# Recurrent layer of a four-layer graph network: two multiplies behind a bank's read, and the output's side steps at other places of length 4

## The chip, the cores and the metric

The kernel runs on one core of a Trainium2 chip. The core has five engines with a queue of instructions each: TensorE (PE, matrix products), VectorE (DVE), ScalarE (ACT), GpSimd (POOL) and SyncE (SP, which here issues nearly all DMA transfers). The metric is the device time of one execution in microseconds, from three runs of each kernel.

## What is computed

The input x has 128 batch rows of 64 nodes with 256 features, in fp32. Four layers follow each other, each as x = layernorm(x + layer(x)): a graph attention layer, an attention layer over an edge list, a layer with two batch norms, and the recurrent layer, which the change concerns:

```
h = relu(adj @ (x @ Wg0 + bg0)); h = relu(adj @ (h @ Wg1 + bg1))
for p in 1..4:
    wins = h in windows of p nodes            # nw = 64 // p windows per batch row
    LSTM p (zero initial state) over the p nodes of each window
    h[last node of each window] = the LSTM's last hidden state
x = layernorm(x + h)
```

An LSTM step is i, f, g, o = x_t @ Wih.T + h @ Whh.T + bias; c = sigmoid(f)*c + sigmoid(i)*tanh(g); h = sigmoid(o)*tanh(c). In length p there are p steps, and the first has no f and no h. "Length 4" is p = 4: four steps of 16 windows. It writes only the last node of each window of four, so nodes 0, 1 and 2 of each window are final before length 4 begins.

## The kernel before

**Groups and pairs.** The recurrent layer handles the batch in 8 groups of 16 rows, two groups (n = 0, 1) at a time: four pairs, k = 0 to 3, one after the other. Within a pair, `lstm(k)` runs lengths 1 to 4. The state is transposed (features on partitions), H is the pair's array of hidden values.

**Seven products.** A gate needs a 2 by 2 block product: feature halves by groups. It is done with seven products in place of eight (Strassen's scheme), with sums of weights (in `wx`, `wh`), of inputs (`xs`) and of hidden values (`hs`), the last two made by DVE and POOL. In lengths 2 to 4 each product j of a gate has an input half (`H` or `xs` by `wx`) and a hidden half (`hid` or `hs` by `wh`), which accumulate in one PSUM bank (L1700). "f.6" below is product 6 of gate f. The banks are a ring of six tiles named `l`, reused in the order of their allocation. Each product's result is read out of its bank by `use`: products 1 and 5 by a copy on ACT (L1715, into `kept`), 2 (L1717), 6 (L1719), 7 (L1721), 4 (L1726) and 3 (L1728) by an addition on DVE. Product 7 has two more additions without PSUM (L1723, L1724), on POOL for f, g and i, on DVE for o. A gate takes its products in the order 1, 5, 2, 6, 7, 4, 3; gate f takes 1, 5, 6, 7, 3, 2, 4; gate o takes 1, 5, 2, 6, 7, 3, 4. Then ACT applies sigmoid or tanh (L1733), and `finish` updates the cell (L1610 on POOL for f, L1613 and L1614 on DVE for i).

**A step's end.** Behind gate o come the input halves of the next gate f (products 1, 5, 6, 7, 3, 2, which fill the six banks), the hidden values (L1600) and their sums: L1564 and L1565 on DVE, L1568 and L1569 on POOL. Then gate f's hidden halves.

**Units.** `lstm` is a generator that stops at numbered places ("at" u, and some "gap" and "wait" places beside them). In length 4: 33 and 34 lie behind gates g and i of step 0, 35 at the end of step 0; 36, 37, 38 behind gates f, g, i of step 1, 39 at its end; 40 to 43 the same for step 2; 44 to 46 behind f, g, i of step 3, and 47 at the end. Two kinds of side work are put at units by `put`:

- `final(g, s)` puts out the nodes s = 0, 1, 2 of group g's windows; it has two halves. The first: x3r is loaded, POOL copies from H to `hd` (L1835), DVE transposes in blocks (L1236), SP sends the result to DRAM (`way<-st`, L1239) and back in four transfers (`st<-way`, L1241). The second: DVE adds x3r (L1850) and takes the norm's sums (L95, L96, L85, L98), POOL the power (L86) and the scaling (L100), SP the output (L1860).
- `gcn` makes the next pair's H, in blocks of 11 or so parts: a fetch of z from DRAM with the same kind of transposition, norms, two matrix layers (L1324 with L1326 on DVE and L1328 on ACT, L1336 with L1339 on DVE) and a last part that writes H (neighbour products L1254, L1347 on DVE, L1348 on ACT). Pair 3 has no next pair, and so none of this.

**Order.** All this is traced through `given`, which keeps the instructions of PE, DVE, ACT and POOL in the order written, but for a few neighbours within one part; each engine's queue is that order. SP's order is a scheduler's.

**Length 1.** Each gate is a `Wide` object, for group n; its products share three banks, so product 4 can only accumulate when the read of 7 (`add(room, b, self.first)`) is done. What a gate leaves over is its `tail`, run between the products of the next gate (`seven`): the first part behind product 1, and so on, in the order 1, 6, 5, 2, 3, 7 (o of group 1: 1, 6, 5, 2, 7, 3). `after(m, v)` multiplies: i by g, or o by tanh of the cell into H. Most DVE work of length 1 is shown under one line, L116, that of the helper which calls it.

Of the kernel before, what the change touches and what calls it, by code (L numbers as in the profile page):

```python
# [41 lines left out]
def kernel(ctx: ExitStack, tc: tile.TileContext, i, out):  # L42
# [67 lines left out]
    def given(do, *args, **more):  # L110
        traced = nc.cur_bb.bb.instructions
        first = len(traced)
        with ExitStack() as order:
            for e in latest.values():
                order.enter_context(tc.issue_after(e))
            r = do(*args, **more)  # L116
        for t in traced[first:]:
            if t.engine in (mybir.EngineType.PE, mybir.EngineType.DVE, mybir.EngineType.Activation,
                            mybir.EngineType.Pool):
                latest[t.engine] = t  # L120
        return r
# [8 lines left out]
    with ExitStack() as two:  # L130
# [605 lines left out]
        def hidden(q, m):  # L736
            return Z[q][:, m, :] if m < 2 else Aq(q)[:, (m - 2) * QT:(m - 1) * QT]
# [15 lines left out]
        def put(q, m, p_):  # L753
            nc.scalar.activation(hidden(q, m), p_, AF.Identity, bias=b1[:, m:m + 1])
            nc.vector.bn_stats(st1[:, m, q, :], hidden(q, m))
# [40 lines left out]
        class Seven:  # L796
# [57 lines left out]
            def tail(self):  # L854
                self.product(4)
                yield self.counted(1, 1)
                yield self.counted(1, 0)
                if self.done:
                    self.order(self.done)
# [114 lines left out]
        def load_x2(q):  # L974
            tiles = []
            for a in range(2):
                tiles.append(wx.tile([P, 2, D], F32, name="x2r"))
                nc.sync.dma_start(tiles[a].rearrange("p c d -> p (c d)"), x2_dram[q][:, a * 2 * D:(a + 1) * 2 * D])
            return tiles

        early = {n: load_x2(n) for n in range(2)}
# [110 lines left out]
        rest = late.pop(0).tail()  # L1092
# [37 lines left out]
        rest = late.pop(0).tail()  # L1130
# [101 lines left out]
    def turned(src):  # L1232


        t = work.tile([P, 4, 4, 32], F32, name="st", bufs=ST)
        nc.vector.transpose(t, src.rearrange("p n (j t) -> p j n t", t=32))  # L1236
        o = work.tile([P, 4, 4, 32], F32, name="st", bufs=ST)
        way = dram.tile([P, 4, P], F32, name="way", bufs=4)
        nc.sync.dma_start(way, t.rearrange("p j n f -> p j (n f)"))  # L1239
        for j in range(4):  # L1240
            nc.sync.dma_start(o[j * 32:(j + 1) * 32].rearrange("t i n f -> t i (n f)"),  # L1241
                              way[:, j, :].rearrange("(i t) x -> t i x", t=32))
        return o.rearrange("p i (c m) f -> p c m i f", m=KD)
# [132 lines left out]
    def lstm(pair):  # L1376
# [19 lines left out]
        class Wide:  # L1396
# [71 lines left out]
                if self.name == "i":  # L1468
                    given(nc.scalar.activation, self.t[m][v], self.t[m][v], AF.Tanh)

            def tail(self):
                self.act(0, 1)
                yield
                self.after(0, 0)
                self.after(0, 1)
                yield
                self.product(4)
                self.act(1, 1)
                yield
                self.act(1, 0)  # L1480
                self.tanh(0, 0)
                yield
                self.after(1, 0)
                self.after(1, 1)
                self.tanh(0, 1)
                yield
                self.tanh(1, 1)
                self.tanh(1, 0)

# [10 lines left out]
        def eight(G, rest):  # L1500

            def two(m, v):
                b = lbank([QT])
                for k in range(KD):
                    nc.tensor.matmul(b, G.weight(m, k), half(G.n, k, v), start=k == 0, stop=k == KD - 1)
                return b

            for m in range(2):
                for v in range(2):
                    G.act(m, v, given(two, m, v))  # L1510
                    next(rest, None)
            for _ in rest:
                pass

        def seven(G, rest, order):
            for j in order:
                G.product(j)
                next(rest, None)
            for _ in rest:
                pass  # L1520

        rest = iter(())
        for n in range(2):
            if n == 0:
                given(column_sums, 0)
                yield "begin", 0
            gates = {}
            for name in "gio":
                if (n, name) == (0, "o"):
                    given(column_sums, 1)  # L1530
                G = Wide(name, n, gates)
                if name == "g" and n == 0:
                    eight(G, rest)
                    rest = iter(())
                else:
                    seven(G, rest, (1, 6, 5, 2, 7, 3) if (n, name) == (1, "o") else (1, 6, 5, 2, 3, 7))
                    rest = G.tail()
                if (n, name) == (1, "o"):
                    G.last()
                yield "at", unit  # L1540
                unit += 1
            yield "at", unit
            unit += 1

        for p in range(2, SKIP + 1):
# [197 lines left out]
            for r in range(len(runs)):  # L1743
                if p > 2:
                    yield "gap", unit
                for s in range(p):
                    last = s == p - 1
                    if s == 0:
                        tiles = {}
                        free, rest = late_columns(r)  # L1750
# [12 lines left out]
                    else:  # L1763
                        names = "fgio"
                        for at, n in enumerate(names):
                            G = nxt or Gate(n, r, s, tiles)
# [61 lines left out]
    def final(g, s, pieces=1):  # L1828

        if s == SKIP - 1:  # L1830
            h = lasts.pop(g)
        else:
            h = late.tile([P, 2, KD, P], F32, name="hd", bufs=3)
            for c in range(2):
                nc.gpsimd.tensor_copy(h[:, c].rearrange("p k (w b) -> p k w b", b=GB),  # L1835
                                      Hs[g // 2][:, g % 2].rearrange("p k (c w s) b -> p c k w s b",
                                                                     c=2, s=SKIP)[:, c, :, :, s, :])

        rows = [v[g * GB:(g + 1) * GB].rearrange("b (c w s) d -> s c w b d", c=2, s=SKIP)[s]
                for v in (x3_dram, out_view)]  # L1840
        xr = work.tile([P, 2, D], F32, name="x3r")
        for c in range(2):
            nc.sync.dma_start(xr[:, c, :], rows[0][c])
        for cs in ([(0, 1)] if pieces == 1 else [(0,), (1,)]):
            r = slice(cs[0], cs[-1] + 1)
            if pieces == 1:
                ht = turned(h.rearrange("p c m t -> p (c m) t"))
                yield
                xv = xr.rearrange("p c (m i f) -> p c m i f", m=KD, f=32)
                nc.vector.tensor_add(xv, ht, xv)  # L1850
            else:
                ht = gbank([2, D])
                for c in cs:
                    for k in range(KD):
                        nc.tensor.transpose(ht[:, c, k * P:(k + 1) * P], h[:, c, k], ident)
                nc.vector.tensor_add(xr[:, r], ht[:, r], xr[:, r])
            o = work.tile([P, 2, D], F32, name="st", bufs=ST)
            layernorm(o[:, r], xr[:, r], len(cs), nc.gpsimd)
            for c in cs:
                nc.sync.dma_start(rows[1][c], o[:, c, :])  # L1860
        yield
# [32 lines left out]
    def gap(u):  # L1894
        return "gap", u

    def wait(u):
        return "wait", u

    for k in range(NP):  # L1900
        if k:
            put(k, prepare(weights_of[k, 3]), 8)
            put(k, prepare(weights_of[k, 4]), 23)
        else:
            put(k, prepare(weights_of[k, 4]), 23, 26, 30)
        for n in range(2):
            g = k * 2 + n
            for s in range(SKIP - 1):
                u = 34 + 4 * s + 2 * n
                put(k, final(g, s), u, u + 2)  # L1910
            if k < NP - 1:
                put(k + 1, final(g, SKIP - 1), 9 + n, 12 + n)
        if k < NP - 1:
            put(k, prepare(weights_of[k + 1, 2]), 34)
            for n, keys in enumerate([
                    [9, gap(11), 12, wait(15), 16, gap(18)],
                    [5, 9, 11, 13, 15, 19, wait(22), gap(22), gap(25), 26, gap(29)],
                    [13, 17, 19, 21, 23, 27, wait(33), gap(33), gap(36), 37, 38],
                    [21, 24, 26, 28, 30, 34, gap(40), 41, gap(44), 45, 46]]):
                block = gcn((k + 1) * 2 + n // 2, n % 2, gbank, "hT")  # L1920
                if n == 0 and k:
                    put(k - 1, block, 40, 42, 43)
                    put(k, block, 0, 0)
                elif n == 0:
                    put(k, block, 0, 1, 3, 5, 7)
                put(k, block, *keys)
# [48 lines left out]
```

## Time and profile before

| what | us |
|---|---|
| median of 3 runs | 2053.97 (2053.06 to 2055.26) |
| profiled execution | 2051.53 |
| its span, first to last instruction | 2049.7 |
| TensorE busy | 1943.6 (95%) |
| DVE, ACT, POOL busy | 1256.3, 987.6, 883.8 |
| mean granted TensorE clock | 0.986 of full speed |

The recurrent layer takes from about 797 us to the end, some 312 us for each pair but the first and last (pair 1 from 1133 to 1445 us). A timeline line reads: start, duration, engine, source line, operation, written tile <- read tiles, shapes, count; in brackets the idle time of that engine just before it and who ended it. Lines of a table of waits read: who waited, for whom: us in total, how often, the longest. The name of a line in the profile (L1700) is a line of the kernel; behind the edited places lines of the changed kernel stand four further on, or three.

### The profile page before, as it was taken

What the parts mean: (1) busy time and instruction counts of PE and PEld (TensorE: products, weight loads), DVE (VectorE), ACT (ScalarE), POOL (GpSimd) and SP (SyncE); (2) the same over time, 40 slices, a digit from 0 to 9 for tenths busy, and PEclk for the clock granted to TensorE, in tenths of its full rate; (3) what the DMA queues carried; (4) which work ended last, traced back from release to release, by engine and by line L of the source; (5) the groups of instructions that cost most, each with busy time, mean ns of one, the idle gap of its engine ahead of it and who ended that gap; (6) DMA issues with size and microseconds to landing.
All of it is one profiled execution on the core that took longest, in us unless ns stands there. A gap on an engine that the chain in (4) does not pass through costs nothing.

```text
span 2049.7 us, 31505 instructions
## 1 busy us (share of the span) xinstructions
PE 1943.6 (95%) x11447; PEld 1332.9 (65%) x11447; DVE 1256.3 (61%) x2763; ACT 987.6 (48%) x1892; POOL 883.8 (43%) x1017
## 2 busy tenths in 40 slices
PE   5999999999899989899999999999999999999997
PEld 4666667766454435477677477677577667578685
DVE  7456665564457454765566865556775557764566
ACT  2766667666335633634343644343544333544333
POOL 1123334343345543564545543435443445444264
PEclk8999999999999999999999999999999999999998
DMA  5344443332112125432242243132143032131022
GB/s 134 79 65 68 79 69 54 66 50 39 37 29 60 41 103 171 158 136 98 112 143 85 77 140 139 42 126 91 52 153 120 21 113 65 44 119 78 0 65 70
DMA packets 236539, 173.84 MB, mean 85 GB/s; under 512 B 150624, under 2 KB 213600, under 8 KB 233056
## 3 DMA queue, kind: packets, MB, share of 16 engines
q1 hardware_dynamic: 234528, 169.86, 29.1%
q8 instruction: 90, 1.47, 0.3%
q0 software_dynamic: 1024, 1.05, 0.2%
q10 hardware_dynamic: 832, 0.92, 0.1%
q14 instruction: 65, 0.53, 0.1%
HBM read 110.18 MB, written 61.60 MB: 84 GB/s over the span
## 4 chain that ended last, share of the span: by engine, by line
PE 68%; DVE 17%; ACT 5%; POOL 4%; issue 4%; DMA 1%; SPq 0%; DVEq 0%; POOLq 0%; ACTq 0%
PE l L1700 25%; PE l L1656 7%; PE l L1437 4%; PE pz L820 4%; PE e L346 3%; PE m L318 2%; PE pz L749 2%; PE g L1336 2%; PE m L253 2%; PE m L321 2%; PE z L355 2%; PE pz L1017 2%; PE g L1324 2%; DVE ln_st L95 1%; DVE cell L1614 1%
## 5 line engine op out<-in xcount | busy, mean ns | idle before, releaser
L1700 PE MATMUL l<-xs,wx 128*128 128x256 f32 (+1 forms) x896 | 277.0, 400 | 5.7 <-DVE gate L1719 4.2
L1700 PE MATMUL l<-hs,wh 128*128 128x256 f32 (+1 forms) x896 | 276.5, 399 | 2.9 <-DVE hs L1564 2.1
L1715 ACT ACTIVATE kept<-l 128x256 f32<-128x256 f32 (+1 forms) x224 | 88.6, 402 | 332.2 <-PE l L1700 330.7
L86 POOL TENSOR_TENSOR ln_rs<-ln_rs,mhalf 128x2 f32<-128x2 f32 (+2 forms) x98 | 86.4, 882 | 338.1 <-DVE ln_rs L98 334.9
L1700 PE MATMUL l<-H,wx 128*128 128x256 f32 (+1 forms) x672 | 210.5, 402 | 4.3 <-DVE gate L1728 3.4
L1700 PE MATMUL l<-hid,wh 128*128 128x256 f32 (+1 forms) x672 | 208.8, 399 | 0.0
L1700 PEld LDWEIGHTS l<-xs,wx 128*128 128x128 f32 x896 | 168.6, 190 | 50.7 <-issue 5.8
L1700 PEld LDWEIGHTS l<-hs,wh 128*128 128x128 f32 x896 | 169.2, 190 | 46.8 <-DVE hs L1564 4.7
L1733 ACT ACTIVATE gate<-gate,bias 128x512 f32<-128x512 f32 (+1 forms) x280 | 170.6, 657 | 42.0 <-DVE gate L1724 34.8
L1656 PE MATMUL l<-H,wx 128*128 128x256 f32 (+5 forms) x672 | 185.2, 431 | 4.9 <-DVE H L116 2.7
L1656 PEld LDWEIGHTS l<-H,wx 128*128 128x128 f32 x672 | 118.8, 190 | 65.5 <-issue 34.2
L357 ACT ACTIVATE u<-z 128x1024 f32<-128x1024 f32 x128 | 130.3, 1025 | 63.4 <-PE z L355 62.6
L1700 PEld LDWEIGHTS l<-H,wx 128*128 128x128 f32 x672 | 125.7, 190 | 42.6 <-DVE gate L1728 7.4
L1700 PEld LDWEIGHTS l<-hid,wh 128*128 128x128 f32 x672 | 127.2, 190 | 32.0 <-issue 2.6
L1723 POOL TENSOR_TENSOR gate<-gate,kept 128x256 f32<-128x256 f32 (+1 forms) x84 | 64.9, 773 | 154.2 <-DVE kept L1721 153.9
L329 DVE TENSOR_TENSOR qs<-m,qs 64x256 fp32r<-64x256 f32 x128 | 54.1, 422 | 109.1 <-ACT qs L328 107.0
L355 PE MATMUL z<-gath_r,qs 128*128 128x512 f32 x256 | 99.9, 478 | 0.6 <-ACT u L357 0.4
L1622 ACT ACTIVATE gate<-cell 128x512 f32<-128x512 f32 (+1 forms) x88 | 58.6, 666 | 86.5 <-DVE cell L1614 64.5
L1568 POOL TENSOR_TENSOR hs<-hid 128x256 f32<-128x256 f32 (+1 forms) x28 | 27.4, 977 | 168.3 <-DVE hid L1600 85.2
L1728 DVE TENSOR_TENSOR gate<-l,gate 128x256 f32<-128x256 f32 (+1 forms) x112 | 50.0, 446 | 61.4 <-POOL gate L1723 36.4
L1610 POOL TENSOR_TENSOR cell<-gate,cell 128x512 f32<-128x512 f32 (+1 forms) x56 | 75.4, 1367 | 28.4 <-ACT gate L1733 28.4
L1717 DVE TENSOR_TENSOR gate<-l,kept 128x256 f32<-128x256 f32 (+1 forms) x112 | 49.2, 439 | 57.1 <-ACT gate L1733 32.9
(375 smaller groups left out, 4095.3 us busy)
## 6 DMA issues: line engine op xcount, KB each, us to landing
wx<-sums SPq DMA_DIRECT2D x9, 2048.0 KB
wh<-sums SPq DMA_DIRECT2D x9, 1792.0 KB
way<-st SPq DMA_DIRECT2D x54, 256.0 KB
st<-way SPq DMA_DIRECT2D x216, 64.0 KB
xin<-in_x SPq DMA_DIRECT2D x16, 512.0 KB
ld<-table SPq DMA_DIRECT2D x16, 512.0 KB
x_dram<-y SPq DMA_DIRECT2D x16, 512.0 KB
x2r<-x_dram SPq DMA_DIRECT2D x32, 256.0 KB
```

Source lines behind the costliest of these rows:

```text
L86: nc.gpsimd.tensor_tensor(dst, dst, mhalf[:, :n], OP.pow)
L346: nc.tensor.matmul(pes[S][n * CG:(n + 1) * CG, :], apad[:, k, CG - HEADS - r0:2 * CG - HEADS - r0], u[:, k, :], start=r0 == 0 and k == 0, ...
L355: nc.tensor.matmul(z[:, k, :], L1[q]["qs"][c][:, s, k * P:(k + 1) * P], gath_r, start=True, stop=True)
L357: nc.scalar.activation(u, z, AF.Relu)
L820: nc.tensor.matmul(self.bank[at], lhs, rhs, start=first and n == 0, stop=n == len(self.terms) - 1, skip_group_check=True)
L1437: nc.tensor.matmul(self.bank[at], lhs, rhs, start=new, stop=True, skip_group_check=True)
L1610: nc.gpsimd.tensor_tensor(c, t, c, OP.mult)
L1656: nc.tensor.matmul(b, w.raw[0][:, k, at, m, :], x, start=k == 0, stop=k == KD - 1)
L1700: nc.tensor.matmul(self.banks[j], lhs, rhs, start=src == 0, stop=src == 1)
L1715: nc.scalar.activation(self.keep(j), b, AF.Copy)
L1723: e.tensor_tensor(t[0][:, 1], t[0][:, 1], k[5], OP.add)
L1733: given(lambda: nc.scalar.activation(dst, dst, f, bias=b))
```

## The change

In length 1, `tail` gets an argument. For every gate but i of group 1, the two multiplies `after(1, 0)` and `after(1, 1)` move from the fifth part (behind product 3 of the next gate) to the sixth (behind product 7, so behind the read of it). For gate g they do nothing; for i of group 0 they are the products i*g, for o of group 0 the writes of H.

In length 4, the places of the side steps change. The halves of `final`, by group n and node s:

| block | first, second half before | after |
|---|---|---|
| n = 0, s = 0 | 34, 36 | 33, 35 |
| n = 1, s = 0 | 36, 38 | 35, 37 |
| n = 0, s = 1 | 38, 40 | 36, 39 |
| n = 1, s = 1 | 40, 42 | 39, 41 |
| n = 0, s = 2 | 42, 44 | 40, 43 |
| n = 1, s = 2 | 44, 46 | 43, 44 |

The last part of the third `gcn` block of the next pair moves from 38 to 39, and the two fetches of the first block of the pair after that from 42 and 43 to 43 and 45. No instruction is added or removed.

```diff
-            def tail(self):
+            def tail(self, early):
                 self.act(0, 1)
                 yield
                 self.after(0, 0)
@@
                 self.act(1, 0)
                 self.tanh(0, 0)
                 yield
-                self.after(1, 0)
-                self.after(1, 1)
+                if early:
+                    self.after(1, 0)
+                    self.after(1, 1)
                 self.tanh(0, 1)
                 yield
+                if not early:
+                    self.after(1, 0)
+                    self.after(1, 1)
                 self.tanh(1, 1)
                 self.tanh(1, 0)
@@
-                    rest = G.tail()
+                    rest = G.tail((n, name) == (1, "i"))
@@
             for s in range(SKIP - 1):
-                u = 34 + 4 * s + 2 * n
-                put(k, final(g, s), u, u + 2)
+                put(k, final(g, s), *((33, 35), (35, 37), (36, 39), (39, 41), (40, 43), (43, 44))[2 * s + n])
@@
-                    [13, 17, 19, 21, 23, 27, wait(33), gap(33), gap(36), 37, 38],
+                    [13, 17, 19, 21, 23, 27, wait(33), gap(33), gap(36), 37, 39],
@@
                 if n == 0 and k:
-                    put(k - 1, block, 40, 42, 43)
+                    put(k - 1, block, 40, 43, 45)
                     put(k, block, 0, 0)
```

## The prediction

> **What bounds the kernel now.** I read the page first: busy time and the slices.
>
> ```profile
> span 2049.7 us, 31505 instructions
> PE 1943.6 (95%) x11447; PEld 1332.9 (65%) x11447; DVE 1256.3 (61%) x2763; ACT 987.6 (48%) x1892; POOL 883.8 (43%) x1017
> PE   5999999999899989899999999999999999999997
> ```
>
> TensorE sets the time; in the recurrent layer (from 797 us on) nearly every slice is full. So an edit elsewhere counts only where it makes PE wait or ends a wait. Next the table of waits:
>
> ```profile
> DVE st L1236 <- POOL hd L1835: 41.8, 20, 3.3
> PE l L1700 <- DVE gate L1719: 4.2, 6, 1.0
> PE l L1700 <- DVE gate L1728: 3.4, 8, 0.4
> ```
>
> PE's waits in lengths 2 to 4 are a few us in all: little is to be won there. DVE waits 41.8 us for the copies of the output's side steps, at no cost to PE. Why not? The timeline after gate f of step 1, second pair of groups (unit 36):
>
> ```profile
> 1364.97 0.88 DVE L1850 TENSOR_TENSOR x3r<-st,x3r 128x512 f32<-128x512 f32 x1
> 1367.05 0.15 DVE L98 TENSOR_SCALAR ln_rs<-ln_mv 128x2 f32<-128x2 f32 x1
> 1367.87 0.70 POOL L86 TENSOR_TENSOR ln_rs<-ln_rs,mhalf 128x2 f32<-128x2 f32 x1
> 1368.67 1.09 POOL L100 TENSOR_SCALAR st<-x3r,ln_rs 128x256 f32<-128x256 f32 x2
> 1369.70 0.74 POOL L1835 COPY hd<-H 128x256 f32<-128x256 f32 x2
> 1370.47 0.71 DVE L1236 STREAM_TRANSPOSE st<-hd 128x512 f32<-128x512 f32 x1 [3.27 <-POOL hd L1835]
> ```
>
> Here one output block's second half (add, norm) is followed by the next block's first half (copies, transpose). DVE sends its sums to POOL, POOL does power, scaling, copies, and DVE stands until the copies end. From L86 to the transpose is 2.6 us. PE goes on because all six `l` banks are filled in turn and gate g's products are ahead of DVE; DVE's next read (g.2, product 2 of g) ends about 1371.5, and PE wants that bank for i.5 at 1372.63. The margin is about 1 us. In the last pair the same place already costs PE 0.49 us.
>
> The step end of step 1 (unit 39):
>
> ```profile
> 1389.60 0.42 DVE L1564 TENSOR_TENSOR hs<-hid 128x256 f32<-128x256 f32 x1
> 1390.06 0.83 DVE L1565 TENSOR_TENSOR hs<-hid,hs 128x256 f32<-128x256 f32 x1
> 1390.96 0.69 DVE L1326 TENSOR_TENSOR hT<-g,rb 128x512 f32<-128x512 f32 x1
> 1391.68 0.63 ACT L1328 ACTIVATE hT<-hT 128x512 f32<-128x512 f32 x1 [2.66 <-DVE hT L1326]
> 1392.22 0.64 ACT L1715 ACTIVATE kept<-l 128x256 f32<-128x256 f32 x2
> 1392.61 0.42 DVE L1719 TENSOR_TENSOR gate<-l,kept 128x256 f32<-128x256 f32 x1 [0.97 <-ACT kept L1715]
> 1393.34 0.59 PE L1700 MATMUL l<-xs,wx 128*128 128x256 f32 x2
> 1395.07 0.60 PE L1700 MATMUL l<-xs,wx 128*128 128x256 f32 x2
> ```
>
> At a step end all six banks hold gate f's input halves, so PE has little to do without readers: f.4 (1393.34) takes f.1's bank, which ACT empties (L1715); g.1 takes f.5's; g.5 (1395.07) takes f.6's, which DVE empties (L1719, done 1393.03). Margin: 2.0 us for DVE, 0.5 us for ACT.
>
> **What the Trainium skill says.** "TensorE: Matmul & The Clock Gate", architectural detail: ACT, DVE and GpSimd queues are strict first in, first out, so an instruction that waits holds all behind it; the 3.27 us above agree. "SBUF — State Buffer", who interferes with whom: DVE and GpSimd share a port pair as a lock; the trace agrees (L1565 takes 0.83 us beside a POOL operation, 0.38 in another place). "DMA: Bandwidth & Descriptors", anatomy of one DMA: about 2 us fixed per transfer; a block's two transfers in a row would be at least 4 us. The trace's number is used: from the transpose's end to landing 7.3 to 8.7 us where x3r loads go between (1371.2 to 1379.9; 2022.2 to 2029.7).
>
> **The change, part by part.**
>
> *Length 1.* Before, DVE does two products i*g (1.3 to 2.2 us) ahead of the read of o.7, and PE waits for that read: 1.12 us in pairs 1 to 3, 0.53 in pair 0. Moved behind it, this wait goes. But ACT's tanh needs the products, and ACT's copy of the next group's g.1 is queued behind tanh; PE needs that copy 1 us later (matmul at 1156.59, copy done 1156.54). The products start 0.35 us later (o.7's 0.68 less the present wait for ACT); bounds 0, where POOL's lock sets their end anyway, and +0.4. I take +0.2 in three pairs and +0.4 in pair 0. The same move for o's products saves in pair 0 alone: PE waits 1.77 us for the add of g.7, which can run 1.5 us earlier. Sum about -0.5 us.
>
> *Length 4, what leaves.* Units 38, 42, 46 (behind gate i) lose their side work, so DVE reaches the cell products sooner. That can end PE's gaps ahead of the step ends: 0.34+0.43 and 0.24+1.02+0.43 us in pair 1, a little less in pairs 0 and 2, 0.46+0.43 and 0.45+0.43 in pair 3. The neighbour products (64 records, 1.16 us) moved from unit 38 to 39 cost PE the same there; their two writes of H go along, L1347 on DVE and L1348 (1.06 us) on ACT, whose only reader is the next pair. The first block for the pair after next moves its two fetches from 42 and 43 to 43 and 45: at 43 the same L1268, L1236 and transfers as now, at 45 another, read two gates and seven us of length 1 later: nothing. In the tail DVE waits 1.14 us for a landing and does 1.9 us of norm ahead of L1613; L1613 can then start when ACT's gate is ready, 2030.9 instead of 2031.74: -0.8.
>
> *Length 4, what arrives.* In the changed program's order, units 35, 39 and 43 have on DVE: L1564, the add L1850 (ahead of L1565 at 39 and 43), statistics, the transpose L1236, and only then gate f's reads; on POOL: power, scaling, copies, and only then L1723 of f.7. The double block that waited behind f now stands ahead of f.
>
> Unit 39, pair 1. DVE's chain comes up to 2.4 us earlier (neighbours gone from 38, no side work): L1564 at 1387.2. Then L1850 to 1388.3, L1565 to 1389.1, statistics 1.55 us to 1390.65, POOL to transpose 2.6 us, transpose to 1394.0, L1347 (the block's write of H, moved here) to 1394.9, L1326 to 1395.6. ACT's L1328 needs L1326 and stands ahead of the copies of f.1 and f.5: 0.63+0.38, 1396.6. PE wants f.1's bank at 1393.34-0.8 = 1392.5: it stands 4.1 us, and after the 0.8 gained the net is +3.3.
>
> Unit 35, pair 1: L1565 done 1359.16; add and statistics to 1361.4; transpose 1364.1 to 1364.8; L1339 to 1365.4; f.6 read at 1365.85. PE wants it at 1364.86: +1.0, and 0.1 where POOL is late for f.3: +1.1. Nothing on ACT waits here.
>
> Unit 43, pair 1: chain 1.6 us earlier, L1564 at 1418.1; L1850, L1565 to 1419.7; statistics 1421.2; transpose 1423.9 to 1424.6; L1236 of that block's fetch and L1339 to 1426.0; f.6 read 1426.4. PE wants it at 1425.16-1.7 = 1423.5: 2.9, net +1.2. Then unit 44: the second half of the block whose first half was at 43. Only the five reads of f lie between, done at 1429; the landing is due 7.3 to 8.7 us after 1424.6, 1431.9 to 1433.3. DVE stands there, then add, statistics and g.2: 2.65 us, 1434.5 to 1435.9. PE wants g.2's bank for i.5 at 1434.15: 0.4 to 1.8, taken as 1.1. Net +2.3.
>
> Sum 6.7 us a pair, pairs 0 to 2 alike: 20.1.
>
> Pair 3 has no next layers to fill PE. Unit 33: the transpose comes ahead of L1616, and the copies end at 1952.05 where L1616 now starts 1950.67: hid and hs come 2.1 us later, PE's margin is 1: +1.1, +0.5 for L1565; then f.6 read at 1965.9 for g.5 wanted 1963.4: +2.5; unit 36's own wait +0.6. Together +4.7. Unit 39: g.5 at 1990.9 instead of 1989.30, +1.6, and i.5 at unit 40 +0.5: +2.1. Units 43, 44: +1.6, then landing 2025.2 to 2026.6, g.2 read 2027.9 to 2029.2, i.5 wanted at 2024.45: 3.4 to 4.8, taken as 4.1: +5.7. Tail -0.8. Sum +11.7.
>
> All: -0.5+20.1+11.7 = +31 us on the profiled execution's own 2051.5 us (span 2049.7), 1.5%. The median of runs is 2.5 us above that execution; the same addition gives 2085. DMA issues are the same in number; SP's order moves with them, and its issue times (0.3 to 0.65 us) lie inside the landings used.
>
> **The rivals.**
> A, faster: the bank ring covers the step ends as it covers unit 36 now, and the gaps ahead of them vanish: about -2 us in each of four pairs, -0.8 in the tail, -0.5 in length 1: -9, 2045. It decides at f.6 read less than 2.0 us later and ACT's copies less than 0.5 us later. For it: 41.8 us of DVE waits cost PE almost nothing today. Against: I count 3.3 to 5.9 us.
> B, small loss: statistics and POOL overlap more than in my chain, and unit 44's landing comes in time. Only the ACT wait at 39 (3.3 x 3) and half of pair 3 (6) remain: +16, 2070.
> C, large loss: transfers land late behind each other and L1339's buffer waits for an output's DMA at 43; 1.5 us more at each of 12 step ends: +49, 2103.
> D, no change: gains and stalls cancel, 2054.
>
> **How the numbers follow.** Forecast 0.56, B 0.22, C 0.10, A 0.08, D 0.04. A measurement tells a change from none at about 0.2%, 4 us. Faster 0.08, same 0.04, slower 0.88. The range leaves out A and D and the far half of C: 2058 to 2102. The likeliest case alone: 2074 to 2096.
>
> **What would show it.** Right: PE gaps behind every step end of length 4, at f.4 (released by ACT L1715) in unit 39 of the first three pairs, at g.5 (by DVE L1719) elsewhere; DVE waiting for L1835 ahead of gate f; DVE waiting for st<-way in unit 44, 1 to 5 us; 1.12 us before o.4 gone, with a wait for ACT at g.2 in its place. Wrong: PE without gaps over 1 us behind the step ends, or the new losses sitting in another length.

## The result, and the profile after

The changed kernel takes 2090.99 us (median of 4 runs, 2088.02 to 2095.23) against 2054.48 us of the kernel before beside it, 36.5 us more. Their ratio was measured as 1.0183, with a 95% interval of 1.017 to 1.0196. On 2051 us that ratio is 37.5 us, and the table of the experiments below reckons every ratio so. The prediction said 2085 (2058 to 2102). The profiled execution has a span of 2086.2 us, 36.5 more than before.

The page of the kernel after, its first lines:

```profile
span 2086.2 us, 31516 instructions
PE 1953.2 (94%) x11447; PEld 1338.5 (64%) x11447; DVE 1256.5 (60%) x2763; ACT 988.7 (47%) x1892; POOL 876.3 (42%) x1017
PE   5999999998999989899999999999999999999986
```

The slices look as before: a loss of 1.8% doesn't show in tenths. One number does: DVE, ACT and POOL are as busy as before within 8 us, yet TensorE's busy time grew by 9.6 us, with the same matmuls. Some of them became slower. We come back to that.

The stages, taken from the first matmul of each in the two traces: length 1 is as long as before in pair 0 and takes 40.3 instead of 39.2 us in each of pairs 1 to 3 (+3.3); lengths 2 and 3 are unchanged; length 4 takes 109.6, 109.4, 108.1 and 113.7 us instead of 100.6, 100.9, 100.0 and 105.6 (+33.7). That is 37.0, less 0.2 us ahead of the layer and rounding.

The table of waits of the kernel after (who waited for whom: total us, times, longest):

```profile
DVE st L1236 <- POOL hd L1839: 68.6, 24, 3.4
PE l L1704 <- DVE gate L1723: 15.1, 9, 4.5
PE l L1437 <- ACT wh L116: 11.0, 5, 3.1
DVE x3r L1854 <- DMA st<-way: 9.6, 4, 4.0
PE l L1704 <- ACT kept L1719: 7.0, 3, 2.3
DVE st L1339 <- DMA out<-st: 3.7, 2, 2.1
PE g L1324 <- ACT H L1348: 3.6, 3, 1.2
```

All 24 transpositions of outputs now wait for POOL's copies. The other rows are PE's and DVE's new waits: 15.1 us for the read of f.6 (L1723; 4.2 before), 7.0 for ACT's copies (no such row before), 3.6 before products of the graph layer, which the prediction had put at nothing, and 11.0 for ACT in length 1 (0.9 before). That last one was forecast in kind, as the wait for ACT at g.2, but its net price was put at 0.2 to 0.4 us a pair. Two of DVE's own are for transfers. Taken one by one, PE's waits of over 0.1 us in the recurrent layer sum to 58.5 us, where they were 31.0.

Unit 39 of pair 1, timeline of the kernel after:

```profile
1398.46 1.05 ACT L1348 ACTIVATE H<-g 128x512 f32<-128x512 f32 x1 [1.36 <-PE g L1254]
1399.57 1.98 PE L1324 MATMUL g<-hT,wg 128*128 128x512 f32 x4 [1.20 <-ACT H L1348]
...
1403.35 0.71 DVE L1236 STREAM_TRANSPOSE st<-hd 128x512 f32<-128x512 f32 x1 [2.62 <-POOL hd L1839]
1404.81 0.66 DVE L1326 TENSOR_TENSOR hT<-g,rb 128x512 f32<-128x512 f32 x1
1405.51 0.63 ACT L1328 ACTIVATE hT<-hT 128x512 f32<-128x512 f32 x1 [6.00 <-DVE hT L1326]
1406.04 0.64 ACT L1719 ACTIVATE kept<-l 128x256 f32<-128x256 f32 x2
...
1406.46 0.70 PE L1704 MATMUL l<-xs,wx 128*128 128x256 f32 x2 [2.32 <-ACT kept L1719]
```

Read it from the bottom: PE stands 2.32 us for ACT's copy of f.1; ACT stood behind L1328, that behind DVE's L1326, that behind the transposition (and L1347, the moved write of H, 0.97 us between them, not shown), and the transposition 2.62 us for POOL's copies. This is the predicted chain, link by link. Ahead of it is another wait of 1.20 us: the neighbour products have filled both `g` banks, and the next user of one, L1324, waits for ACT to read it (L1348).

Unit 43 of pair 1, same view:

```profile
1436.50 0.71 DVE L1236 STREAM_TRANSPOSE st<-hd 128x512 f32<-128x512 f32 x1 [2.62 <-POOL hd L1839]
1437.14 0.67 DVE L1236 STREAM_TRANSPOSE st<-A 128x512 f32<-128x512 f32 x1
1439.95 0.69 DVE L1339 TENSOR_TENSOR st<-g,bg 128x512 f32<-128x512 f32 x1 [2.14 <-DMA out<-st]
1440.56 0.41 DVE L1723 TENSOR_TENSOR gate<-l,kept 128x256 f32<-128x256 f32 x1
...
1441.03 1.22 PE L1704 MATMUL l<-xs,wx 128*128 128x256 f32 x2 [4.53 <-DVE gate L1723]
1442.04 1.06 PE L1704 MATMUL l<-hs,wh 128*128 128x256 f32 x2
```

Here DVE waits twice: for the copies, and then, with the sum L1339 in hand, 2.14 us for a free tile of `st`, a ring of five tiles: the store of an output, whose second half was issued 1.2 us before, still reads it. So f.6 is read 4.5 us late. And after the stall a pair of matmuls takes 1.06 us from the first's start to the second's end, where such pairs took 0.59. The windows of that place (columns: stretch, length, busy us and records of PE, PEld, DVE, ACT, POOL, granted clock, DMA share, GB/s):

```profile
1431.90:1435.30 3.40, 3.40 (x18) 2.89 (x17) 1.94 (x8) 0.77 (x2) 2.03 (x4) 1.00 0.00 0
1435.30:1438.70 3.40, 1.20 (x6) 0.72 (x4) 1.30 (x2) 0.38 (x1) 1.17 (x3) 1.00 0.33 93
1438.70:1442.10 3.40, 1.07 (x3) 0.89 (x4) 1.45 (x3) 0.00 (x0) 0.45 (x1) 0.50 0.41 141
1442.10:1445.50 3.40, 3.40 (x10) 2.68 (x9) 1.85 (x5) 2.29 (x5) 0.97 (x2) 0.50 0.49 157
1445.50:1448.90 3.40, 3.40 (x17) 3.01 (x16) 2.65 (x10) 0.41 (x1) 2.11 (x4) 1.00 0.23 68
```

PEclk goes to 0.50 for 6.8 us and comes back. In the fourth stretch PE is busy throughout with 10 records where the first has 18. In the kernel before the clock stays at 1.00 from 777 to 2037 us, near the end; after the change it is 0.50 in four places, 20.5 us together. In the recurrent layer PE's busy time grew by 8.9 us; 7.6 of these are 36 matmuls that start 0.43 us apart there instead of 0.216. So 27.5 us of waits and 8.9 us of longer busy time make 36.4 of the 36.5 us.

Length 1 of pair 1, first before, then after:

```profile
1152.63 2.24 DVE L116 TENSOR_TENSOR wh<-wh,hs 128x512 f32<-128x512 f32 x2 [0.19 <-ACT wh L116]
1155.53 1.12 PE L1437 MATMUL l<-wx,wih 128*128 128x512 f32 x2 [1.12 <-DVE gate L116]
1155.62 1.27 POOL L116 TENSOR_TENSOR gate<-gate 128x512 f32<-128x512 f32 x1 [1.90 <-DVE gate L116]
```

```profile
1161.58 2.98 DVE L116 TENSOR_TENSOR wh<-wh,hs 128x512 f32<-128x512 f32 x2
1162.30 1.71 POOL L116 TENSOR_TENSOR gate<-gate 128x512 f32<-128x512 f32 x1
1164.59 1.15 ACT L116 ACTIVATE wh<-wh 128x512 f32<-128x512 f32 x2 [2.34 <-DVE wh L116]
1165.65 0.58 ACT L116 ACTIVATE wh<-l 128x512 f32<-128x512 f32 x1
...
1166.28 1.12 PE L1437 MATMUL l<-H,wih 128*128 128x512 f32 x2 [2.40 <-ACT wh L116]
```

The wait of 1.12 us before o.4 is gone. In its place PE waits 2.40 us before product 2 of the next group's gate g: the products i*g take 2.98 us instead of 2.24, then comes tanh, then ACT's copy of g.1. POOL's addition behind o.7, which stood behind the products before, now runs beside them.

### The profile page after: what moved, and what is told of

Same layout as the page of the kernel before. It is cut to its first block, busy times and chain, and to the rows that moved or that the text cites. A ratio compares the mean times of both kernels' runs of the same rounds, so it can differ in the third digit from the quotient of the medians.

```text
span 2086.2 us, 31516 instructions
## 1 busy us (share of the span) xinstructions
PE 1953.2 (94%) x11447; PEld 1338.5 (64%) x11447; DVE 1256.5 (60%) x2763; ACT 988.7 (47%) x1892; POOL 876.3 (42%) x1017
## 4 chain that ended last, share of the span: by engine, by line
PE 67%; DVE 17%; ACT 5%; POOL 5%; issue 4%; DMA 2%; SPq 0%; DVEq 0%; POOLq 0%; ACTq 0%
PE l L1704 26%; PE l L1660 7%; PE l L1437 5%; PE pz L820 4%; PE pz L749 3%; PE e L346 3%; PE m L318 2%; PE pz L1017 2%; PE g L1336 2%; PE z L355 2%; PE m L321 2%; PE g L1324 2%; PE m L253 1%; DVE cell L1618 1%; PE l L1509 1%
## 5 line engine op out<-in xcount | busy, mean ns | idle before, releaser
L1704 PE MATMUL l<-xs,wx 128*128 128x256 f32 (+1 forms) x896 | 279.7, 404 | 26.8 <-DVE gate L1723 15.1
L1719 ACT ACTIVATE kept<-l 128x256 f32<-128x256 f32 (+1 forms) x224 | 88.6, 402 | 359.6 <-PE l L1704 358.3
L86 POOL TENSOR_TENSOR ln_rs<-ln_rs,mhalf 128x2 f32<-128x2 f32 (+2 forms) x98 | 85.0, 868 | 340.7 <-DVE ln_rs L98 338.3
L355 PE MATMUL z<-gath_r,qs 128*128 128x512 f32 x256 | 100.6, 480 | 0.6 <-issue 0.4
```

The source lines that it names most:

```text
L86: nc.gpsimd.tensor_tensor(dst, dst, mhalf[:, :n], OP.pow)
L355: nc.tensor.matmul(z[:, k, :], L1[q]["qs"][c][:, s, k * P:(k + 1) * P], gath_r, start=True, stop=True)
L1704: nc.tensor.matmul(self.banks[j], lhs, rhs, start=src == 0, stop=src == 1)
L1719: nc.scalar.activation(self.keep(j), b, AF.Copy)
```

## The experiments

Two theories stood at the start. The first is the prediction's, sharpened by the trace: copies of POOL that DVE has to await, now ahead of gate f's reads, plus the ring of five tiles at 43 and the clock behind long stalls. The rival: the cost lies in the meeting of moved graph-layer work and moved outputs, or in something at step ends as such, and the named waits merely cover another.

All ratios are to the kernel before, run on the same chip (its median 2054.5 beside after, 2050.4 to 2051.0 beside the others). The column "us" is the ratio's distance from 1, times 2051 us. "Waits" is the sum of PE's waits of over 0.1 us in the recurrent layer, "half clock" the time at 0.50 there ahead of the tail, both of the profiled execution.

| kernel | ratio (95%) | us | waits | half clock |
|---|---|---|---|---|
| before | 1 | | 31.0 | 0 |
| after | 1.0183 (1.017 to 1.0196) | +37.5 | 58.5 | 20.5 |
| length 1 alone | 1.0034 (1.0022 to 1.0046) | +7.0 | 35.5 | 10.2 |
| length 4 alone | 1.016 (1.0144 to 1.0175) | +32.8 | 55.9 | 17.1 |
| graph layer's keys alone | 1.0017 (1.0011 to 1.0024) | +3.5 | 35.4 | 0 |
| outputs' places alone | 1.0215 (1.02 to 1.0231) | +44.1 | 60.1 | 34.1 |
| after, one store left out | 1.0168 (1.0153 to 1.0184) | +34.5 | 54.9 | 23.9 |
| after, early copies | 1.0114 (1.0099 to 1.013) | +23.4 | 49.1 | 23.9 |
| after, one start at 40 | 1.017 (1.0154 to 1.0185) | +34.9 | 55.7 | 23.9 |
| early copies, store left out | 1.0079 (1.0064 to 1.0094) | +16.2 | 43.4 | 17.1 |
| length 1 alone, no addition | 1.0005 (0.9997 to 1.0014) | +1.0 | 31.7 | 3.4 |
| after, all mended | 0.9987 (0.9981 to 0.9994) | -2.7 | 29.0 | 0 |
| before, early copies | 0.9981 (0.9973 to 0.9989) | -3.9 | 29.2 | 0 |
| before, early copies, late fetches | 1.0003 (0.9994 to 1.0011) | +0.6 | 32.0 | 0 |

### The change in parts

Length 1 alone: the changed `tail` on the places of before.

```
-                    rest = G.tail()
+                    rest = G.tail((n, name) == (1, "i"))
```

> The kernel before with the new order of the products i*g and o's reads in length 1 alone. From the two traces: pairs 1 to 3 lose 1.1 us each in length 1 and pair 0 nothing, so +3.3 us, 2057.8 us; the wait of TensorE before o.4 is gone and one of 2.4 us stands before product 2 of the next group's gate g, because POOL's add of o.7 now runs beside VectorE's products and these take 3.0 us instead of 2.2. As the prediction had it: -0.5 us, 2054.0 us. Rival: the order in length 1 costs nothing by itself and the 1.1 us come with the other work of the changed kernel: 2054.5 us.

Measured +7.0 us, twice what the two traces gave. The trace has the forecast wait of 2.40 us, and more; the windows around it:

```profile
1153.60:1157.00 3.40, 1.44 (x3) 0.59 (x4) 1.70 (x4) 3.12 (x6) 0.00 (x0) 1.00 0.00 0
1157.00:1160.40 3.40, 3.40 (x5) 1.35 (x4) 1.91 (x4) 1.52 (x3) 0.00 (x0) 0.50 0.00 0
1160.40:1163.80 3.40, 3.40 (x9) 1.52 (x8) 3.39 (x4) 1.72 (x4) 1.58 (x1) 1.00 0.00 0
```

In this execution 2.0 us of the wait lie in one stretch of 3.4 us and leave PE 1.44 us of work, and the next stretch runs at half clock, 5 records instead of 9. The like happened in all of pairs 1 to 3. In the profiled execution of after, the same wait of 2.40 us fell across two stretches and cost no clock. So the price of this edit is 1.1 us a pair without the clock and about 2.6 with it (41.7 to 42.0 us for length 1 instead of 39.2).

Length 4 alone: all moves of side steps, the old `tail`.

```
-                    rest = G.tail((n, name) == (1, "i"))
+                    rest = G.tail(True)
```

> The kernel after with the old order in length 1: only the side steps of length 4 are moved. If the parts add up: 2091.0 less 3.3, 2087.7 us, and stages of length 4 of 109.5, 109.5, 108 and 113.7 us. If the prediction's sizes were right for each part: 2085.5 us. Rival: later side steps of a pair and the next pair's length 1 disturb each other, and the parts don't add up: outside 2085 to 2090.

+32.8 us; with length 1 alone that makes 39.8 where both together give 37.5. The sum lies inside the interval of after (34.9 to 40.2 us), so the two parts add up within what is measured.

Graph layer's keys (the places given to `put`) alone, and outputs' places alone:

```
-                    [13, 17, 19, 21, 23, 27, wait(33), gap(33), gap(36), 37, 38],
+                    [13, 17, 19, 21, 23, 27, wait(33), gap(33), gap(36), 37, 39],
...
-                    put(k - 1, block, 40, 42, 43)
+                    put(k - 1, block, 40, 43, 45)
```

> The kernel before with only the graph layer's keys moved (its last neighbours to unit 39, the fetches of A to 43 and 45). From the trace of after: TensorE waits 1.2 us before the products with wg behind unit 39, since both g banks are still held by the neighbours, in pairs 0 to 2, +3.6 us, less up to 1 us per pair of waits behind units 38 and 42 that lose this work: +1 to +4 us, 2055.5 to 2058.5 us, and no wait of VectorE's add of bg for a transfer of an output, since at the old places the five tiles before it are a unit older. As the prediction had it: nothing for the neighbours, at most -1 us: 2053.5 us. Rival: the move of A to 43 alone brings the wait on the ring and some 4 us in pairs 0 and 1: over 2061 us.

```
-                u = 34 + 4 * s + 2 * n
-                put(k, final(g, s), u, u + 2)
+                put(k, final(g, s), *((33, 35), (35, 37), (36, 39), (39, 41), (40, 43), (43, 44))[2 * s + n])
```

> The kernel before with only the output's side steps moved. From the trace of after: all of length 4's loss but the 1.2 us before the products with wg, 33.5 less 3.6, so about 2084 us; the waits of 2.3 us before f.4 in unit 39 and of 4 us before g.5 in unit 43 are there, with the halved clock behind the latter. Rival: the loss needs both moves, since the graph layer's steps and the output's meet in units 39 and 43: under 2075 us.

The keys alone cost 3.5 us, as the trace theory had it, with the wait for ACT at unit 39 in all of pairs 0 to 2. Timeline of that run, pair 1:

```profile
1389.29 1.04 ACT L1348 ACTIVATE H<-g 128x512 f32<-128x512 f32 x1 [1.37 <-PE g L1254]
...
1390.37 1.98 PE L1324 MATMUL g<-hT,wg 128*128 128x512 f32 x4 [1.18 <-ACT H L1348]
```

The outputs alone cost 44.1 us, more than everything together: my 2084 was wrong. The rival that the loss needs both moves falls with it. On the outputs' new places, the graph layer's new keys save some 11 us. Timeline of this run at units 39 and 43 of pair 1 (its lines are numbered as before the change, so L1715 and L1719 are ACT's copies and the read of f.6):

```profile
1408.01 1.22 PE L1700 MATMUL l<-xs,wx 128*128 128x256 f32 x2 [4.00 <-ACT kept L1715]
...
1444.89 0.69 DVE L1339 TENSOR_TENSOR st<-g,bg 128x512 f32<-128x512 f32 x1 [3.12 <-DMA way<-st]
...
1445.97 1.22 PE L1700 MATMUL l<-xs,wx 128*128 128x256 f32 x2 [5.50 <-DVE gate L1719]
```

With the neighbour products left at 38, PE's wait at 39 is one piece of 4.00 us instead of 1.20 and 2.32 apart, and behind this piece the clock was halved in all of pairs 0 to 2; in after, that happened behind unit 39 in pair 2 alone. At 43 DVE waits 3.12 us for a tile instead of 2.14, and for a later transfer: one more fetch of A (at 42 and 43) has taken its tiles from the ring by then, where in after only the one at 43 has. (That reason is read from the program, not tried by itself.)

### Copies and ring

After, without the stores of the third step's first output:

```
             for c in cs:
-                nc.sync.dma_start(rows[1][c], o[:, c, :])
+                if (s, g % 2) != (2, 0):
+                    nc.sync.dma_start(rows[1][c], o[:, c, :])
```

> The kernel after without the stores of one of a pair's six outputs (length 4's third step, first group), which leaves those rows of the result unwritten. It is the store for which VectorE's add of bg waits 2.1 us behind unit 43. If that wait, and the halved clock behind it, are what unit 43 costs beyond the prediction's 2.9 us: in pairs 0 and 1 TensorE's wait before g.5 falls from 4.0 and 4.5 to 1.7 to 2.4 us, as it is in pair 2 without the wait, the granted clock stays at 1.0 there, and the time falls by 2 x (2.1 + 2.2), about 8.6 us. If the clock falls for other reasons than this wait: by 4 us only. Rival: the ring isn't the cause, VectorE waits as long for another tile: no gain, within 1.5 us of after. After is taken as 33 us + 4.5 us above before on this chip.

The same place in its trace:

```profile
1435.68 0.71 DVE L1236 STREAM_TRANSPOSE st<-hd 128x512 f32<-128x512 f32 x1 [2.64 <-POOL hd L1839]
...
1436.91 0.65 DVE L1339 TENSOR_TENSOR st<-g,bg 128x512 f32<-128x512 f32 x1
...
1437.95 0.70 PE L1704 MATMUL l<-xs,wx 128*128 128x256 f32 x2 [2.28 <-DVE gate L1723]
```

DVE's wait for the tile is gone and PE's fell from 4.53 to 2.28 us, as expected: the ring is the cause of that piece. The time fell by 3.0 us only (34.5 from 37.5; the two intervals overlap), not by 8.6. Two things are seen in the trace. One gate later PE now waits 0.61 us in pair 0 and 0.99 in pair 1, so its waits fell by 3.5 us in all. And the clock's share of the gain didn't come: the clock was halved for 3.4 us behind this 2.28 us stall all the same in pair 1, and behind stalls at unit 39 (pairs 0 and 1) and in length 1 that had cost no clock in the profiled execution of after; 23.9 us in all. That is one execution of each kernel, so how much of the missing gain is the clock's isn't settled.

After, with the copies for step-end transpositions made at 34, 37 and 41:

```
+            yield
...
-                put(k, final(g, s), *((33, 35), (35, 37), (36, 39), (39, 41), (40, 43), (43, 44))[2 * s + n])
+                put(k, final(g, s), *((33, 33, 35), (34, 35, 37), (36, 36, 39), (37, 39, 41), (40, 40, 43), (41, 43, 44))[2 * s + n])
```

The `yield` stands behind the two copies in `final`, so that a block has three steps: copies, transposition, second half.

> The kernel after, with GpSimd's copies hd for the three transpositions behind step ends (units 35, 39, 43) made at units 34, 37 and 41, so that VectorE finds them ready. If VectorE standing before its transposition for these copies is the cause in units 39 and 43, as the prediction had it: its 2.6 us of waiting there go, with them TensorE's 2.3 us before f.4 in unit 39, and 2 to 2.6 us of the 4.0 and 4.5 us before g.5 in unit 43, and the clock is not halved any more: some 5 us per pair and 2 us of clock in pairs 0 and 1, 15 to 25 us less than after. The 1.2 us before the products with wg stay. Rival: the order of VectorE's own work behind the step end, not the copies, sets the loss: less than 6 us of gain.

14 us of the 37.5 are gone, just under the 15 to 25 expected: for this part of the loss the cause holds. Units 39 and 43 of pair 1:

```profile
1397.72 0.70 DVE L1236 STREAM_TRANSPOSE st<-hd 128x512 f32<-128x512 f32 x1
...
1400.44 0.64 ACT L1719 ACTIVATE kept<-l 128x256 f32<-128x256 f32 x2
...
1435.13 0.69 DVE L1339 TENSOR_TENSOR st<-g,bg 128x512 f32<-128x512 f32 x1 [5.54 <-DMA out<-st]
...
1436.20 1.22 PE L1704 MATMUL l<-xs,wx 128*128 128x256 f32 x2 [5.20 <-DVE gate L1723]
```

At 39 the transposition waits for nothing and f.4 has no wait left. At 43 DVE comes earlier and stands 5.54 us for the tile: one cause taken away leaves the other in full. The forecast missed there (I had expected 2 to 2.6 us less at g.5), and for the clock too, which was at half for 23.9 us here.

Both together, the early copies and the store left out:

> The kernel after with both causes taken away, the early copies of hd and no store of the third step's first output (rows left unwritten). If the copies and the ring of five are what units 39 and 43 cost: the 5.0 and 5.2 us before g.5 in unit 43 of the run with early copies fall under 2 us, too short for the clock, 2 x (3.3 + 2.2) less, about +12 us over before, of which 3.6 the neighbours at 39, some 7 length 1 with its clock. If the transfer is only one of several late things there and another takes its place: +18 to +23 us.

+16.2 us, between the two. PE's wait at g.5 in 43 is down to 0.40 us, but the second half of the block follows one unit later, and its line says what is late next:

```profile
1433.02 0.69 DVE L1855 TENSOR_TENSOR x3r<-st,x3r 128x512 f32<-128x512 f32 x1 [4.42 <-DMA st<-way]
```

DVE waits for the transposed block to come back from DRAM. PE then stands 1.20 us before i.5 and 1.45 us one gate later. This is the landing at unit 44 that the prediction named; while 43 itself was late it had been partly covered.

After, with one first half moved from 39 to 40:

```
-                put(k, final(g, s), *((33, 35), (35, 37), (36, 39), (39, 41), (40, 43), (43, 44))[2 * s + n])
+                put(k, final(g, s), *((33, 35), (35, 37), (36, 39), (40, 41), (41, 43), (43, 44))[2 * s + n])
```

> The kernel after with one output's first side step moved from the step end 39 to unit 40 (and the next one's from 40 to 41, so that no more than two are open). If the prediction's chain (copies, transposition, VectorE's add L1326, ScalarE's L1328, the copy of f.1) is what holds f.4 in unit 39: the 2.3 us are gone in pairs 0 to 2, as is some of pair 3's wait, 6 to 8 us less than after, unless units 40 and 41 take over a wait. The 1.2 us before the products with wg stay or go with it: they depend on the neighbours at 39 alone, so they stay. Rival: the wait moves one unit on and nothing is gained: within 1.5 us of after.

2.6 us less than after, with overlapping intervals: not the 6 to 8 expected, and by the time alone not to be told from nothing. The trace can tell. At 39 only the 1.20 us remain; the 2.32 us are gone in pairs 0 to 2. At 41, where a double block stands now, the same chain through L1326 and L1328 makes PE wait 1.04, 1.26 and 1.55 us, and in pair 3 the wait at unit 44 grew from 2.48 to 3.70 us. So the wait moved on, in the main:

```profile
1414.21 0.68 DVE L1326 TENSOR_TENSOR hT<-g,rb 128x512 f32<-128x512 f32 x1
...
1415.46 0.64 ACT L1719 ACTIVATE kept<-l 128x256 f32<-128x256 f32 x2
...
1415.88 0.70 PE L1704 MATMUL l<-H,wx 128*128 128x256 f32 x2 [1.26 <-ACT kept L1719]
```

### Length 1: the addition beside the products

Length 1 alone, without GpSimd's addition behind o.7 of the first group:

```
-                    given(nc.gpsimd.tensor_tensor, t[1][1], room, t[1][1], OP.add)
+                    if (self.n, self.name) != (0, "o"):
+                        given(nc.gpsimd.tensor_tensor, t[1][1], room, t[1][1], OP.add)
```

> The kernel with the new order in length 1 alone, without GpSimd's addition behind product 7 of gate o in the first group (the fourth quarter of that gate then lacks a term). If that addition, which now runs beside VectorE's two products i*g, makes them 3.0 us instead of 2.2: they take 2.2 us again, TensorE's wait before product 2 of the next gate g falls from 2.40 to about 1.65 us, too short to halve the clock of the next 3.4 us, and the kernel is 1 to 3 us slower than before where the new order with the addition was 7 us slower. If the products are long for another reason, or what follows them is late anyhow: the wait stays at 2.40 us, the clock is halved in pairs 1 to 3, and 7 us remain.

+1.0 us instead of +7.0, with an interval that takes in no change at all; length 1 takes 39.2 us in pairs 1 to 3, as before. Its timeline, against 3.00 us for the two products and 2.40 of waiting with the addition:

```profile
1152.39 1.91 DVE L116 TENSOR_TENSOR wh<-wh,hs 128x512 f32<-128x512 f32 x2
...
1156.01 1.13 PE L1437 MATMUL l<-H,wih 128*128 128x512 f32 x2 [1.32 <-ACT wh L116]
```

So the addition beside them is what makes the products long, the long products are what stretches PE's wait from 1.32 to 2.40 us, and behind the 1.32 us the clock stays whole in pairs 1 to 3. The Trainium skill agrees: "SBUF — State Buffer", who interferes with whom, says that a DVE instruction with two SBUF inputs contends with a GpSimd instruction that reads SBUF; here it is 1.1 us for two products beside one addition.

### Mended kernels

After with every cause found taken out and nothing left out:

```
-                    rest = G.tail((n, name) == (1, "i"))
+                    rest = G.tail(True)
...
+                put(k, final(g, s), *((33, 33, 35), (34, 35, 37), (36, 36, 39), (37, 39, 41), (40, 40, 43), (41, 43, 45))[2 * s + n])
...
+                    [13, 17, 19, 21, 23, 27, wait(33), gap(33), gap(36), 37, 38],
...
+                    put(k - 1, block, 40, 45, 46)
```

> The kernel after with every cause found mended, nothing left out: early copies of hd, old order in length 1, neighbours back at unit 38, A's two fetches at 45 and 46 so that they hold no tile of the ring at 43, the last output's second step at 45. If the causes are complete, the relief behind units 38, 42 and 46 is all that is left: 1 to 2 us per pair less than before, -2 to -8 us. If steps behind step ends have a further cost of their own: over +3 us. If the stall in unit 43 moves to 44 or 45: 0 to +10 us with a wait of over 1.5 us there.

-2.7 us: it beats before, if narrowly. So the causes found account for the whole loss, taken together; this kernel doesn't try each mend by itself. At 43 nothing waits in pairs 0 to 2. At 39 a rest of 1.28 to 1.59 us is left, so steps behind a step end aren't quite free even with their copies ready; in pairs 0 and 1 the gaps that went behind units 38 and 42 outweigh it, in pair 2 they about match it:

```profile
1393.59 0.70 PE L1704 MATMUL l<-xs,wx 128*128 128x256 f32 x2 [1.28 <-ACT kept L1719]
...
1421.54 0.65 DVE L1339 TENSOR_TENSOR st<-g,bg 128x512 f32<-128x512 f32 x1
```

Before, with all copies made ahead and the places else unchanged:

```
+            yield
...
-                u = 34 + 4 * s + 2 * n
-                put(k, final(g, s), u, u + 2)
+                put(k, final(g, s), *((33, 34, 36), (34, 36, 38), (37, 38, 40), (38, 40, 42), (41, 42, 44), (42, 44, 46))[2 * s + n])
```

> The kernel before with GpSimd's copies hd made up to one unit and a half ahead of each transposition, at units 33, 34, 37, 38, 41 and 42, all else as before. If VectorE's waits for these copies are also what makes TensorE wait behind units 38, 42 and 46 of the kernel before (1.1 to 2 us per pair): -3 to -7 us, a kernel faster than both. If those waits come from VectorE's own additions and statistics there: within 2 us of before. If GpSimd's copies, one unit ahead, now delay its own sums or gate additions: slower than before by 2 to 8 us.

-3.9 us (0.11 to 0.27% less), the lowest ratio of this study, though the interval of the mended kernel overlaps its own. The row of 41.8 us in which DVE waits for the copies no longer exists. In the trace, length 4 is 0.8 to 1.1 us shorter in every one of the four pairs, so the gain lies where the edit is. PE's waits in the whole recurrent layer fell by less, from 31.0 to 29.2 us; between single executions 2 us are not to be told apart.

The same with A's two fetches moved from 42 and 43 to 45 and 46:

```
-                    put(k - 1, block, 40, 42, 43)
+                    put(k - 1, block, 40, 45, 46)
```

> The kernel before with copies of hd ahead of the transpositions, as in the run that was 0.2% faster, and A's fetches at 45 and 46 instead of 42 and 43. If VectorE's load in unit 42 still makes the waits of 0.50 and 0.43 us there: these go, 1 us per pair in pairs 0 and 1: -5 us against before, -1 to -2 against that run. If 45 and 46 have less room than 42: 0 to -2 us against before.

No gain, +0.6 us. The 0.50 us at unit 42 went in both pairs, but in length 1 of the next pair PE waits 1.67 and 2.07 us (pairs 1 and 2) where DVE's and POOL's norms now stand (the trace names POOL's L86 and DVE's L96 as releasers).

## Why the prediction was right, and where its steps were not

The direction, the mechanism and the place were right: a double block ahead of gate f makes DVE stand for POOL's copies where all six `l` banks wait for readers. The forecast's own +31 us stands against +36.5 in the profiled execution. That it came so near is in part luck: pairs 0 to 2 were put at 6.7 us each and cost 9.0, 8.5 and 8.1 in length 4, pair 3 was put at 11.7 and cost 8.1, length 1 was put at -0.5 and cost 3.3, and a cost without a term, the clock, is inside these figures. Terms too large and too small made up for each other. One by one:

- *Length 1, -0.5 us.* Wrong in sign: +3.3 in the trace of after and +7.0 alone. The failed step is "The products start 0.35 us later ... I take +0.2". It looked at when the products start and not at what then runs beside them. As o.7 is read earlier, POOL's addition comes earlier too, and falls on the products; the run without it gives +1.0.
- *What leaves, units 38, 42, 46.* Right in the first three pairs: the gaps there fell to 0.14 us. In pair 3 only the first of each two gaps went; the other, 0.43 us, stayed, and behind it the wait for hs grew from 0.44 to 0.97 us.
- *Unit 35, +1.1.* Over-sized: PE waits 0.32 us.
- *Unit 39, 4.1 us of waiting, ACT's copy of f.1 as the last link.* The chain was right, and its size too where the neighbours stay at 38: 4.00 us. In after the wait is 1.20 + 2.32. The step that failed is that the neighbours "cost PE the same there": their write L1348 "whose only reader is the next pair" also frees one of only two `g` banks, and the next products need it at once. A tile's readers are not the only ones who wait for its last read; the next owner of its buffer does too.
- *Unit 43, 2.9 us at g.5.* In pair 2, where no fetch of A stands there, 1.68 us; in pairs 0 and 1, 3.96 and 4.53. The buffer of L1339 that waits for an output's store was put into rival C with a chance of 0.10. It came true at this one step end, twice, 3.7 us of DVE's time; with it gone PE waits 2.28 us.
- *Unit 44, the landing, 1.1 us net.* Right in kind, changing in place: DVE waits 9.6 us over four of these, PE 2.48 in pair 3, and 1.46 one gate later in pair 2 (how much of that is the landing's was not tried apart). In pairs 0 and 1 PE doesn't wait there. It had just stood 4 us at 43 and run at half clock, and so came late itself; with the early copies and the store left out, PE does wait there (0.40 and 1.20 us), which fits.
- *Pair 3, +11.7.* It was +8.1. The step at unit 33 failed: "the copies end at 1952.05" took 1.20 us for a pair of copies that measured 0.74. Counted from the length's first matmul, L1620 came 1.6 us later than before and not 2.1, the hidden values only 0.9 us later, and PE waits 0.16 us for hs. The wait at g.5 of unit 35 was 1.80 instead of 2.5, those at g.5 of 39 and 43 were 1.08 instead of 1.6, and that at 44 was 2.48 instead of 3.4 to 4.8.
- *The granted clock: no term.* The prediction counted waits alone, 31 us; they came to 27.5 net. The rest is PE's longer busy time, 8.9 us in the trace, most of it matmuls at half clock. No rival had it, A and B least of all. The rival on the other side, A, fell with its own condition: f.6 was read more than 2.0 us and ACT's copies more than 0.5 us later, as counted.

## What to carry to other kernels

An engine's wait that costs next to nothing at one place can cost most of its length at another: 41.8 us of DVE's waits for copies cost some 4 us behind gates with a bank ring ahead of them, and such waits behind the step ends cost some 14 us (after against after with early copies). Before moving a step, list the waits inside it and ask who stands behind each; better, make its slow input earlier so that the step can't wait, which was worth 3.9 us here on places that were thought free. And where a trace shows the clock halved behind stalls, as here from 2 us on, price a stall with the slow matmuls that follow it.

## What the runs showed of the hardware

The clock. In all fourteen traces the changes of the granted clock lie on a grid of 3.41 us, 1.0 or 0.50, nothing between. Cutting the recurrent layer (860 to 2028 us) into that grid and adding up PE's idle time in each cell that itself ran at full clock: of 25 cells with 2.0 us of idle time or more, all 25 were followed by a cell at half clock; of 4720 with less than 1.7 us, none; of 11 between, 2. So in these traces it is the idle time in a fixed cell that counts, not the length of a stall: a wait of 2.40 us halved the clock when 2.0 to 2.4 us of it lay in one cell (length 1 alone, three times) and did not when it fell across two (after, three times). Where the cells begin differs from trace to trace, so the same wait pays in one and not in another. The four runs of after fit this: the fastest (2088.0 us) has the highest mean granted clock, 0.982, and the slowest (2095.2 us) has 0.980. Where each of them lost its clock isn't on record.

"TensorE: Matmul & The Clock Gate" of the Trainium skill, part 1, what's actually happening, has the free-running window of 3413 ns and the two states, which these traces bear out. Its advice further down (why this matters for your kernels), no idle gaps over about 3 us between bursts, is too mild for this kernel: 2.0 us of idle time within a window were enough. The measurement decides.
